# Edge keys kept by feature and turned back, over a longer look-ahead, in a graph attention kernel

## The chip, the cores and the metric

One NeuronCore of a Trainium2 chip runs the whole program. The metric is device time in microseconds (us); less is better. The kernel before took 2671.06 us as the median of three runs (2661.86 to 2672.03).

## The reference, cut to what matters

There are 12500 nodes and 212500 directed edges, sorted by their target node, each with 128 features in float32. Eight heads of 16 features work side by side.

```python
h = jnp.maximum(_layernorm(x, axis=-1), 0.0)
q = (h @ Wq.T + bq).reshape(N, 8, 16)
k = (edge_h @ Wk.T + bk).reshape(-1, 8, 16)          # one k per edge
v = (h @ Wv.T + bv).reshape(N, 8, 16)
qs, qd = q[src], q[dst]
in_m, out_m, diag_m = (jnp.sum(a * b, axis=-1) for a, b in ((qs, k), (qd, k), (qs, qd)))
score = (_segment_softmax(in_m * SCALE, dst, N) + _segment_softmax(out_m * SCALE, dst, N)
         + _segment_softmax(diag_m * SCALE, dst, N)) * distance ** lam
out = segment_sum(score[..., None] * v[dst], dst, N).reshape(N, 128) @ Wo.T + bo
x = x + leaky_relu(out, negative_slope=0.1)
```

## The kernel before, in words

Everything here is in `ordered_path`. A short first stage normalizes the nodes and writes a table of q. Then a loop runs over 415 turns (`for g in range(end)`, L1694), each on 512 edges: 4 edges on each of 128 partitions. Five turns make a step: `s = g % 5`, `t = g // 5`, 83 steps. After the loop a short tail finishes the last nodes. The helper `pin` ties every instruction to the one recorded before it on its engine, so the order of the calls in the program is the order on each engine, and a wait of one instruction holds up all that stand behind it there.

In turn g the work that this change touches is the following.

- `fetch_edges` (L692, queue of SyncE, SP): loads the edge features of one turn, 256 KB, into one of six buffers `ea`, six turns ahead.
- `turn(g + 2)`: TensorE (PE) transposes the four 128x128 blocks of `ea` into PSUM (`eT_ps`, one buffer, L1266); ScalarE (ACT) copies them to `eT` in SBUF (L1268). Features now lie on the partitions.
- `one_hots(g + 3)`: two ACT operations (L703, L704) make the selection matrix `oh` for the targets.
- `project(g + 1)`: four matmuls, each with one block of `eT` as the weights and Wk moving (L1274), and one matmul of three rows that adds bk in bfloat16 parts (L1275), fill `k_ps` (two buffers). Edges lie on the partitions again.
- `spread_q(g + 1)`: four bfloat16 matmuls take the targets' q from a window of the table by `oh` (L1282) into `qd_ps` (two buffers); ACT copies it to `qd` (L1285).
- `logits(g)`: VectorE (DVE) multiplies `qq` by `k_ps` (L1293), `qq` by `qd_ps` (L1294), `qd` by `k_ps` (L1295), and reduces over each head's 16 features (L1296).
- `gather(g + 26)` (L712, GpSimd, called POOL): four indirect DMAs fetch the sources' q into `qq`, 64 KB each. The first of the four waits for the PE instruction noted as `behind[.., 0]`, the last one of `project` a turn earlier; the third waits for `behind[.., 2]`, the last that PE was given in the earlier turn.

Behind these each turn carries a piece of older steps' work, by `s`: transposes of the logits (`turn_head`, `turn_logits`, L1316, L1324), running maxima on DVE (L1356, L1363, L1384) and their transposes (`turn_max`, L1396), exponentials (L1405, L1406, L1424), the selection `sel` (L1438 to L1442), sums per node (`to_rows`, L1452, L1457) and their stores on SP (L1473), and some node work (L1197 to L1241). Below this is called the small work of a turn. `fetch_rows` (L686) loads the window of q; `fetch` (L665, L670) loads 630 KB and 135 KB once a step.

PSUM has eight banks: `eT_ps` 1, `k_ps` 2, `qd_ps` 2 and 3 shared by the small work (`small`).

## Time and profile before

| what | value |
|---|---|
| median of three runs | 2671.06 us |
| profiled execution | 2660.3 us |
| its span, first to last instruction | 2658.5 us |
| mean granted TensorE clock | 0.756 |
| PE busy | 71% of the span |
| weight loads (PEld) busy | 55% |
| DVE busy | 76% |
| ACT busy | 53% |
| POOL busy | 60% |
| mean traffic to and from HBM | 134 GB/s |

A group row of the profile reads: line, engine, operation, what it writes and reads, shape, count; then busy time in us and the mean of one in ns; then how long the engine sat idle just before these instructions, and what ended most of that. PE is the row of matmuls, PEld that of the weight loads that overlap them. The ends of matmuls are modelled and not measured, so their durations overlap. "Remote" as the end of a wait means that the profile names no instruction for it, and "issue" that it shows no wait at all.

### The profile page before, as it was taken

The numbers are of one execution on the slowest core, as the hardware profiler recorded it, in microseconds if no ns is written. First come the engines' busy times: TensorE is split into PE (matmuls) and PEld (weight loads), VectorE is DVE, ScalarE is ACT, GpSimd is POOL, SyncE is SP. The second block draws the span as 40 slices with busy tenths as digits, with TensorE's granted clock in tenths as the row PEclk, the third lists the DMA queues.
The fourth block names the chain that finished last, engine by engine and source line by source line (L and its number), as shares of the span: only waits on it lengthen the run. The fifth ranks groups of instructions, "written<-read, shape, count | busy, mean of one in ns | idle before, by whom it ended". The sixth has DMA issues, their size and how long they took to land.

```text
span 2658.5 us, 37037 instructions
## 1 busy us (share of the span) xinstructions
PE 1895.1 (71%) x10956; PEld 1466.7 (55%) x10956; DVE 2032.3 (76%) x2813; ACT 1406.8 (53%) x2743; POOL 1584.0 (60%) x1680
## 2 busy tenths in 40 slices
PE   4657866677677767777777767767767687777785
PEld 2446655555455555555555556545655565555564
DVE  4648878777777877777778777777877777777995
ACT  3647745554455555554555555545555555554672
POOL 6655666666666666666666666666666666666100
PEclk6777877776777777777777777777777777677886
DMA  7655445445545555455445444554455445454431
GB/s 197 191 163 150 127 133 143 129 135 139 146 131 144 134 147 135 136 141 141 119 130 139 128 129 130 135 137 122 123 140 135 127 127 135 134 131 122 126 88 53
DMA packets 379583, 357.03 MB, mean 134 GB/s; under 512 B 193216, under 2 KB 299371, under 8 KB 379167
## 3 DMA queue, kind: packets, MB, share of 16 engines
q1 hardware_dynamic: 310637, 239.38, 32.5%
q0 software_dynamic: 53152, 108.92, 16.4%
q10 hardware_dynamic: 15584, 6.27, 1.0%
q8 instruction: 90, 1.47, 0.2%
q14 instruction: 120, 0.98, 0.1%
HBM read 322.10 MB, written 32.22 MB: 133 GB/s over the span
## 4 chain that ended last, share of the span: by engine, by line
PE 48%; issue 14%; ACT 14%; DVE 12%; another core or an unknown queue 10%; DMA 1%; DVEq 1%; POOL 0%; SPq 0%; ACTq 0%
PE k_ps L1274 13%; PE eT_ps L1266 8%; PE w_ps L1452 6%; PE qd_ps L1282 4%; PE k_ps L1275 4%; ACT eT L1268 3%; ACT qd L1285 2%; PE m_ps L1396 2%; DVE lT L1296 2%; PE node_ps L1205 2%; ACT relb L703 2%; DVE prod L1294 2%; DVE prod L1293 1%; PE d_ps L1438 1%
## 5 line engine op out<-in xcount | busy, mean ns | idle before, releaser
L712 POOL DMA_INDIRECT qq<-q_table,sources x1564 | 1480.3, 946 | 852.7 <-issue 355.1
L1296 DVE TENSOR_REDUCE lT<-prod 128x96 f32<-128x1536 f32 x415 | 727.5, 1753 | 14.3
L1274 PE MATMUL k_ps<-wk,eT 128*128 128x128 f32 x3320 | 613.6, 343 | 70.5 <-issue 41.0
L1274 PEld LDWEIGHTS k_ps<-wk,eT 128*128 128x128 f32 x3320 | 562.0, 254 | 99.0 <-issue 54.2
L1266 PE MATMUL eT_ps<-ident,ea 128*128 128x128 f32 x1660 | 352.7, 347 | 349.7 <-issue 226.9
L1285 ACT COPY qd<-qd_ps 128x512 f32<-128x512 f32 x415 | 239.4, 577 | 533.7 <-remote 164.3
L1266 PEld LDWEIGHTS eT_ps<-ident,ea 128*128 128x128 f32 x1660 | 243.5, 177 | 441.1 <-issue 269.5
L1293 DVE TENSOR_TENSOR prod<-qq,k_ps 128x512 f32<-128x512 f32 x412 | 280.5, 681 | 186.6 <-remote 55.4
L1268 ACT COPY eT<-eT_ps 128x512 f32<-128x512 f32 x415 | 242.7, 585 | 252.9 <-remote 125.2
L1294 DVE TENSOR_TENSOR prod<-qq,qd_ps 128x512 f32<-128x512 f32 x412 | 281.4, 683 | 100.8 <-ACT qd L1285 55.0
L703 ACT ACTIVATE relb<-relb,before 126x512 bf16<-126x512 bf16 x415 | 302.6, 729 | 0.0
L1295 DVE TENSOR_TENSOR prod<-qd,k_ps 128x512 f32<-128x512 f32 x415 | 282.2, 680 | 0.0
L1452 PE MATMUL w_ps<-back,sel 128*126 128x144 f32 (+1 forms) x1296 | 209.5, 325 | 95.0 <-ACT sel L1442 59.2
L704 ACT ACTIVATE oh<-relb 126x512 bf16<-126x512 bf16 x415 | 261.4, 630 | 13.2
L1452 PEld LDWEIGHTS w_ps<-back,sel 128*126 128x126 f32 (+1 forms) x1296 | 190.7, 218 | 106.0 <-ACT sel L1442 66.2
L1282 PE MATMUL qd_ps<-win,oh 126*128 126x128 bf16 x1660 | 194.8, 248 | 12.6 <-issue 12.4
L1275 PE MATMUL k_ps<-b,ones 3*128 3x512 bf16 x415 | 192.6, 464 | 4.7 <-issue 4.7
L1282 PEld LDWEIGHTS <-oh 126*128 126x128 bf16 x1660 | 109.2, 107 | 141.7 <-issue 141.4
L1405 DVE TENSOR_TENSOR back<-lT,m_ps 128x480 f32<-128x480 f32 x83 | 54.1, 651 | 98.3 <-remote 37.7
L1356 DVE TENSOR_TENSOR_SCAN l_ps<-far,carry,l_ps 120x512 f32<-120x512 bf16 x80 | 102.5, 1282 | 20.1 <-PE h_ps L1324 10.2
L1396 PE MATMUL m_ps<-ident,m 120*128 120x120 f32 x332 | 72.4, 349 | 52.7 <-issue 38.1
L712 POOL DMA_INDIRECT qq<-in_x_dram,sources x84 | 81.7, 973 | 42.8 <-issue 22.2
(237 smaller groups left out, 1811.1 us busy)
## 6 DMA issues: line engine op xcount, KB each, us to landing
ea<-in_edge_attr_dram SPq DMA_DIRECT2D x415, 256.0 KB
relb<-rel_d SPq DMA_DIRECT2D x83, 630.0 KB
qq<-q_table,sources POOLq DMA_INDIRECT x1564
win<-q_table SPq DMA_DIRECT2D x415, 31.5 KB
far<-far_d SPq DMA_DIRECT2D x84, 135.0 KB
q_table<-q SPq DMA_DIRECT2D x24, 384.0 KB
sums<-rows SPq DMA_DIRECT2D x411, 7.9 KB
q_table<-xq SPq DMA_DIRECT2D x24, 256.0 KB
```

Of the source, the lines that this page charges most:

```text
L703: pin(nc.scalar.activation(d, d, AF.Abs, bias=before[:K3]))
L712: rows = pin(nc.gpsimd.indirect_dma_start(out=qq[:, j, :], out_offset=None, in_=x if g < RAW else q_table, in_offset=bass.IndirectOffsetOn ...
L1266: pin(nc.tensor.transpose(eT_ps[:, j, :], eas[g][:, j * F:(j + 1) * F], ident))
L1268: pin(nc.scalar.copy(eT, eT_ps))
L1274: pin(nc.tensor.matmul(k_ps[:, j, :], eTs[g][:, j, :], wk, start=(j == 0), stop=False))
L1275: pin(nc.tensor.matmul(k_ps, ones3, bk3, start=False, stop=True))
L1282: pin(nc.tensor.matmul(qd_ps[:, j, :], ohs[g][:, j * P:(j + 1) * P], d["win"][:, s, :], start=(j == 0), stop=(j == JN - 1)))
L1285: pin(nc.scalar.copy(qds[g], qd_ps))
L1293: pin(nc.vector.tensor_mul(prod[:, :, 0, :], qqs[g], ks[g]))
L1294: pin(nc.vector.tensor_mul(prod[:, :, 1, :], qqs[g], q_ps[g]))
L1296: pin(nc.vector.tensor_reduce(lTs[t][:, :, s, :], prod.rearrange("p j i (h d) -> p j (i h) d", d=DIM), AX.X, ALU.add))
L1452: pin(nc.tensor.matmul(w_ps[:(hi - lo) * W, lo:hi].rearrange("p s c -> p (s c)"), d["sel"][:n, j, lo:hi, :].rearrange("p s w -> p (s w)"), ...
```

## The change

Wk stays in the array as the weights, and the transposed edge features move through it, 512 columns in one matmul. The product is k by feature (`kT_ps`); ACT adds bk as a bias per partition while it copies it to SBUF (`kT`), and PE transposes it back into `k_ps` (`turn_back`). In turn g PE now does `turn_back(g + 1)`, `spread_q(g + 1)`, `project(g + 3)`, `turn(g + 4)` and then the small work. `kT_ps` takes one PSUM bank, and `qd_ps` has one buffer in place of two; the product with `qd_ps` comes first in `logits`. `behind[.., 0]` is now the last instruction of `spread_q`. `eT` has two buffers in place of three. The edge features come in two loads a step, one of three turns (768 KB) and one of two turns (512 KB), with one buffer each, called seven turns ahead, behind `turn(g + 4)`.

```diff
+    bk_col = consts.tile([P, 1], F32, name="bk_col")
+    pin(nc.scalar.dma_start(bk_col, bk[:, None]))
...
+    EA = {0: 3, 3: 2}
...
-    AHEAD, IDX, EDGES = LOOK + FIRST, 8, 6
+    AHEAD, IDX, EDGES = LOOK + FIRST, 8, 7
...
     def fetch_edges(g):
-        if g < end:
-            ea = eas[g] = load.tile([P, JN * F], F32, name="ea", bufs=EDGES)
+        if g < end and g % S in EA:
+            n = EA[g % S]
+            ea = load.tile([P, n, JN * F], F32, name=f"ea_{n}", bufs=1)
+            for i in range(n):
+                eas[g + i] = ea[:, i]
             pin(nc.sync.dma_start(
                 ea, edge_attr[:end * BE, :].rearrange("(s b p j) f -> p s b (j f)", s=S, b=G, p=P)
-                [:, g % S, g // S, :]))
+                [:, g % S:g % S + n, g // S, :]))
...
-            eT = work.tile([P, JN, P], F32, name="eT", bufs=3)
+            eT = work.tile([P, JN, P], F32, name="eT")
...
         def project(g):
+            kT_ps = ps.tile([P, JN, P], F32, name="kT_ps", bufs=1)
+            pin(nc.tensor.matmul(kT_ps.rearrange("f j p -> f (j p)"), wk,
+                                 eTs.pop(g).rearrange("f j p -> f (j p)"), start=True, stop=True))
+            kTs[g] = work.tile([P, JN, P], F32, name="kT", bufs=3)
+            pin(nc.scalar.activation(kTs[g], kT_ps, AF.Identity, bias=bk_col))
+
+        def turn_back(g):
             k_ps = ks[g] = ps.tile([P, JN, F], F32, name="k_ps", bufs=2)
             for j in range(JN):
-                pin(nc.tensor.matmul(k_ps[:, j, :], eTs[g][:, j, :], wk, start=(j == 0), stop=False))
-            pin(nc.tensor.matmul(k_ps, ones3, bk3, start=False, stop=True))
-            del eTs[g]
+                pin(nc.tensor.transpose(k_ps[:, j, :], kTs[g][:, j, :], ident))
+            del kTs[g]
...
-            qd_ps = q_ps[g] = ps.tile([P, JN, F], F32, name="qd_ps", bufs=2)
+            qd_ps = q_ps[g] = ps.tile([P, JN, F], F32, name="qd_ps", bufs=1)
...
+            pin(nc.vector.tensor_mul(prod[:, :, 1, :], qqs[g], q_ps[g]))
             pin(nc.vector.tensor_mul(prod[:, :, 0, :], qqs[g], ks[g]))
-            pin(nc.vector.tensor_mul(prod[:, :, 1, :], qqs[g], q_ps[g]))
...
         for g in range(end):
...
-            fetch_edges(g + EDGES)
             if s == 1:
                 load_sources(t + IDX)
-            if g + 2 < end:
-                turn(g + 2)
-            one_hots(g + 3)
             if g + 1 < end:
-                project(g + 1)
+                turn_back(g + 1)
+                one_hots(g + 3)
+                spread_q(g + 1)
                 behind[g + 1, 0] = pinned[products]
-                spread_q(g + 1)
+            if g + 3 < end:
+                project(g + 3)
+            if g + 4 < end:
+                turn(g + 4)
+            fetch_edges(g + EDGES)
             logits(g)
```

What it does to the order on the engines is shown at three places; line numbers in rows of the changed kernel are its own. On PE before, from the last part of one `spread_q` through the next turn's transposes of `ea` and its `project` into the next `spread_q`:

```order
L1282 LDWEIGHTS oh_12237
L1282 MATMUL qd_ps_12355<-win_11957,oh_12237 128x128
L1266 MATMUL eT_ps_12378<-ident_75,ea_12166 128x128 x4
L1274 MATMUL k_ps_12388<-wk_94,eT_12344 128x128 x4
L1275 LDWEIGHTS ones3_90
L1275 MATMUL k_ps_12388<-b3_96,ones3_90 128x512
L1282 LDWEIGHTS oh_12291
L1282 MATMUL qd_ps_12394<-win_11957,oh_12291 128x128
```

The `eT` that `project` reads was transposed one turn earlier, and the transposes into the one `eT_ps` stand ahead of it. On PE now, at a like place in a turn whose small work is `show_ends` (L1450):

```order
L1294 LDWEIGHTS oh_12460
L1294 MATMUL qd_ps_12551<-win_12054,oh_12460 128x128
L1279 MATMUL kT_ps_12558<-eT_12521,wk_96 128x512
L1272 MATMUL eT_ps_12562<-ident_75,ea_3_12297 128x128 x4
L1450 LDWEIGHTS ends_t1_113
L1450 MATMUL d_ps_12577<-shows_111,ends_t1_113 128x420
L1287 MATMUL k_ps_12608<-ident_75,kT_12514 128x128 x4
L1294 LDWEIGHTS oh_12502
L1294 MATMUL qd_ps_12616<-win_12328,oh_12502 128x128
```

`spread_q` (L1294) moved ahead of the transposes of `ea` (L1272), and what DVE needs of k (L1287) is read from a `kT` that was projected two turns earlier. On ACT before, from one copy of `qd` to the next, in a turn with the exponential (L1406) and node work (L1186) in it:

```order
L1285 COPY qd_9714<-qd_ps_9709 128x512
L1406 ACTIVATE back_9726<-back_9726 128x20x24
L1186 ACTIVATE h_9731<-x_in_9640,shift_98,inv_97 128x128 x2
L1268 COPY eT_9746<-eT_ps_9741 128x512
L703 ACTIVATE relb_9516<-relb_9516,before_88 126x512
L704 ACTIVATE oh_9748<-relb_9516 126x512
L1285 COPY qd_9762<-qd_ps_9757 128x512
```

And on ACT now, through one turn:

```order
L709 ACTIVATE relb_8415<-relb_8415,before_90 126x512
L710 ACTIVATE oh_8656<-relb_8415 126x512
L1297 COPY qd_8664<-qd_ps_8659 128x512
L1282 ACTIVATE kT_8668<-kT_ps_8666,bk_col_78 128x512
L1274 COPY eT_8675<-eT_ps_8670 128x512
L1453 ACTIVATE sel_8684<-d_ps_8685 128x420
```

Three copies out of PSUM now follow each other, and the small work stands behind the copy of `eT` in place of ahead of it. On the queue of SP now, in a turn with s = 3, where the load of three turns stands (before, a load of one turn stood in every turn, ahead of the window `win` and the stores of `sums`):

```order
L689 DMA win_10662<-q3_table_62 126x128
L1485 ISA
L1485 DMA sums3_68<-rows_10713 42x48
L698 DMA ea_3_10928<-in_edge_attr_128_dram 128x3x512
L668 DMA relb_10944<-rel_d_63 126x5x512
L673 DMA far_10946<-far_d_64 120x1x576
L675 TENSOR_LOAD places_120
```

The load of `ea_3` waits for the transposes of the same turn, and the once-a-step loads of `fetch` queue behind it.

More of the change, by code (lines that the diff above doesn't have):

```diff
@@ L1690, in ordered_path @@
         project(0)
+        turn(1)
+        turn_back(0)
         spread_q(0)
-        turn(1)
+        project(1)
+        turn(2)
+        project(2)
+        turn(3)
+        fetch_edges(S)
         raw_rectify(SOON)
@@ L1810, in ordered_path @@
             halves_of(ab, engine)
[L1811 to L1813 removed]
+        places_o = [ps.tile([P, JN, F], F32, name=name, bufs=n) for name, n in
+                    (("eT_ps", 1), ("kT_ps", 1), ("k_ps", 2), ("k_ps", 2), ("qd_ps", 1))]
         for r in range(len(rest) + 2):
```

9 lines of the change are left out of this document (3 added, 6 removed).

## The prediction, made before the changed kernel was timed

> **What bounds the kernel now.** I read the busy rows of the page first, then the same by stretches, with and without the gathers of POOL.
>
> ```profile
> PE 1895.1 (71%) x10956; PEld 1466.7 (55%) x10956; DVE 2032.3 (76%) x2813; ACT 1406.8 (53%) x2743; POOL 1584.0 (60%) x1680
> ```
>
> No engine is full over the span. The stretches say more. The first view counts the reduces of `logits` (L1296), one for each turn; the second shows what all engines do in the same stretches.
>
> ```profile
> 300.00:1350.00 1050.00, 312.04 (x178) 0.75 0.52 137
> ...
> 2480.00:2590.00 110.00, 42.07 (x24) 0.86 0.36 101
> ```
>
> ```profile
> 300.00:1350.00 1050.00, 756.79 (x4325) 578.79 (x4323) 817.44 (x1018) 545.11 (x1037) 671.63 (x710) 0.75 0.52 137
> ...
> 2480.00:2590.00 110.00, 92.84 (x627) 73.52 (x627) 107.69 (x136) 80.55 (x163) 1.67 (x4) 0.86 0.36 101
> ```
>
> A turn takes 1050/178 = 5.90 us while POOL gathers and 110/24 = 4.58 us once the gathers are over. In the later stretch DVE is busy for 107.69 of 110 us: there DVE is the bound. In the earlier one DVE is busy for 817.44/178 = 4.59 us of 5.90 and PE for 4.25 us: some 1.3 us a turn are waits, over about 390 turns 510 us. Who waits is in the rows of the page's costliest groups and, for POOL, in the first of them.
>
> ```profile
> L712 POOL DMA_INDIRECT qq<-q_table,sources x1564 | 1480.3, 946 | 852.7 <-issue 355.1
> ...
> L1274 PE MATMUL k_ps<-wk,eT 128*128 128x128 f32 x3320 | 613.6, 343 | 70.5 <-issue 41.0
> L1274 PEld LDWEIGHTS k_ps<-wk,eT 128*128 128x128 f32 x3320 | 562.0, 254 | 99.0 <-issue 54.2
> L1266 PE MATMUL eT_ps<-ident,ea 128*128 128x128 f32 x1660 | 352.7, 347 | 349.7 <-issue 226.9
> L1285 ACT COPY qd<-qd_ps 128x512 f32<-128x512 f32 x415 | 239.4, 577 | 533.7 <-remote 164.3
> L1266 PEld LDWEIGHTS eT_ps<-ident,ea 128*128 128x128 f32 x1660 | 243.5, 177 | 441.1 <-issue 269.5
> L1293 DVE TENSOR_TENSOR prod<-qq,k_ps 128x512 f32<-128x512 f32 x412 | 280.5, 681 | 186.6 <-remote 55.4
> L1268 ACT COPY eT<-eT_ps 128x512 f32<-128x512 f32 x415 | 242.7, 585 | 252.9 <-remote 125.2
> L1294 DVE TENSOR_TENSOR prod<-qq,qd_ps 128x512 f32<-128x512 f32 x412 | 281.4, 683 | 100.8 <-ACT qd L1285 55.0
> ...
> L1282 PE MATMUL qd_ps<-win,oh 126*128 126x128 bf16 x1660 | 194.8, 248 | 12.6 <-issue 12.4
> L1275 PE MATMUL k_ps<-b,ones 3*128 3x512 bf16 x415 | 192.6, 464 | 4.7 <-issue 4.7
> ```
>
> PE's one large wait stands ahead of the transposes into `eT_ps`: 349.7 us. ACT waits 533.7 us ahead of the copy of `qd` and 252.9 us ahead of the copy of `eT`, and DVE 186.6 + 100.8 = 287.4 us ahead of its first two products. The timeline of one turn shows how they hang together.
>
> ```profile
> 1517.82 0.60 PE L1282 MATMUL qd_ps<-win,oh 126*128 126x128 bf16 x4
> ...
> 1518.21 1.06 PE L1266 MATMUL eT_ps<-ident,ea 128*128 128x128 f32 x4
> ...
> 1518.84 0.94 POOL L712 DMA_INDIRECT qq<-q_table,sources  x1 [0.30 <-issue]
> ...
> 1521.05 0.69 PE L1396 MATMUL m_ps<-ident,m 120*128 120x120 f32 x4
> ...
> 1522.42 0.69 DVE L1293 TENSOR_TENSOR prod<-qq,k_ps 128x512 f32<-128x512 f32 x1 [1.92 <-PE m_ps L1396]
> 1522.48 0.59 ACT L1285 COPY qd<-qd_ps 128x512 f32<-128x512 f32 x1 [4.44 <-PE m_ps L1396]
> 1522.66 0.94 POOL L712 DMA_INDIRECT qq<-q_table,sources  x1 [1.63 <-PE m_ps L1396]
> ...
> 1522.96 0.59 ACT L1268 COPY eT<-eT_ps 128x512 f32<-128x512 f32 x1
> ...
> 1523.61 1.12 PE L1266 MATMUL eT_ps<-ident,ea 128*128 128x128 f32 x4 [1.86 <-ACT eT L1268]
> ```
>
> By the records `spread_q` ends at 1518.42, but its copy starts at 1522.48, with ACT idle for 4.44 us: what PE has done reaches DVE, ACT and POOL some 4 us late, and to all three at once. Then ACT copies `eT`, and only then can PE transpose again. This lateness goes with the gathers. The copy of `qd` by stretches, first the one with gathers, then the one without:
>
> ```profile
> L1285 ACT COPY qd<-qd_ps 128x512 f32<-128x512 f32 x355 | 205.1, 578 | 493.9 <-remote 138.8 <-PE qd_ps L1282 78.3 <-PE m_ps L1396 76.0
> ...
> L1285 ACT COPY qd<-qd_ps 128x512 f32<-128x512 f32 x24 | 13.7, 570 | 1.6 <-PE qd_ps L1282 1.5
> ```
>
> 493.9/355 = 1.39 us of idle a turn against 1.6/24 = 0.07 us. The trace doesn't say why PE's releases come late while gathers run; I take it as given. The loop is then a round of late releases, PE to ACT to PE, and looser couplings should shorten it.
>
> **The change part by part.** Times are those of the profiled execution, 2660.3 us with a span of 2658.5.
>
> *PE's work.* It loses the rows of L1274 and L1275, 613.6 + 192.6 = 806.2 us. It gains 415 x 4 transposes, by the row of L1266 352.7 us, and 415 matmuls of 512 columns, in two records each. The nearest row is a float32 matmul of that shape:
>
> ```profile
> L1572 PE MATMUL rest_ps<-q_in,ident 128*128 128x512 f32 (+1 forms) x34 | 21.2, 712 | 2.9 <-issue 2.5 <-ACT hT L1200 0.4
> ```
>
> 21.2/34 = 0.62 us a record gives 830 x 0.62 = 515 us. Net: 515 + 353 - 806 = +62 us. If a record takes its whole 0.712 us it is +138, if the bias matmul's overlap was worth nothing it is about 0. Weight loads fall by 562.0 us and gain 243.5 and some 160, but they overlap and are no term. PE's share of the chain that ended last is this:
>
> ```profile
> PE 48%; issue 14%; ACT 14%; DVE 12%; another core or an unknown queue 10%; DMA 1%; DVEq 1%; POOL 0%; SPq 0%; ACTq 0%
> ```
>
> At 48% the +62 cost 30 us; bounds 0 and 138.
>
> *ACT's work.* 415 more copies at 0.585 us (L1268): +243 us, 53% to 62% of the span. They lie beside other work except where PE or DVE wait for ACT; at ACT's 14% of the chain that is +34 us, bounds 0 and 243.
>
> *The wait ahead of the transposes.* The wait rows of PE have it in two parts.
>
> ```profile
> PE eT_ps L1266 <- issue: 226.9, 132, 7.4
> ...
> PE eT_ps L1266 <- ACT eT L1268: 110.3, 65, 6.3
> ```
>
> 197 waits hold nearly all of 349.7 us: 1.77 us each. Nothing of the next turn may pass them now. After the change PE meets `turn_back` first, whose `kT` was made two turns earlier: 352.7/415 = 0.85 us of work that needs nothing fresh. Then `spread_q` (194.8/415 = 0.47 us), which needs the product and the copy that free the one `qd_ps`, and those come as late as the copy of `eT` did. So I count 0.85 of each 1.77 us as covered and the rest as still there, now ahead of `spread_q`, `project` or `turn`: 197 x 0.85 = -167 us. Bounds: none of it, or both pieces, 197 x 1.32 = -260. What is late next is `qd_ps`.
>
> *Edits at nothing.* The new order of the three products costs nothing, as all three are done before the reduce; it frees `qd_ps` one product earlier. A load fewer in three of five turns on SP's queue saves nothing (SPq is 0% of the chain). The load of three turns waits on SP for the transposes of its own turn, with `relb`, `far`, the window and the stores behind it; the transposes that need it stand three turns later, 3 x 5.90 = 17.7 us, which hide it. If that cover goes, PE waits for the load (a rival below). `eT` with two buffers: its reader is one turn behind, so 0. POOL's first gate moves from behind `project` to behind `spread_q`, one piece earlier in PE's turn: taken as 0, at best a part of POOL's wait. `bk_col` is one small load at the start: 0.
>
> Sum: -167 + 30 + 34 = -103, so 2557 for the profiled execution. The median of the runs lies 10.8 us above that execution: **2568 us**. About 0.5% (13 us) is what a measurement of this kernel can tell from no change.
>
> **A rule that speaks against it.** Rows first: the clock was 0.75 in the stretch where PE was busy for 72% and 0.86 where it was for 84%. The Trainium skill ("TensorE: Matmul & The Clock Gate", Part 4: PE-mode transpose) holds that work in transpose mode does not count as activity for the gate, so that the full clock is not granted for it. By that rule this change, which swaps matmuls for transposes, would lower the clock; the trace shows the clock rising with PE's busy share, but no stretch with transposes alone.
>
> **The rivals.**
>
> *The gain is larger.* `turn_back` and `spread_q` both run ahead of the late releases, PE is never the one waited for, and DVE's waits shrink too: -260 + 30 + 34 = -196, so 2475. For it: DVE has 4.59 us of work in 5.90, and POOL's own pace, 946 ns (L712) and 0.30 us between two gathers (the timeline's row of 1518.84), is 4 x 1.25 = 5.0 us a turn. Against it: the single `qd_ps`. Chance 0.15.
>
> *The clock falls.* The clock goes down to half in stretches of some us:
>
> ```profile
> 1513.20:1519.90 6.70, 6.14 (x30) 5.19 (x30) 5.75 (x9) 4.42 (x10) 4.72 (x5) 0.50 0.54 158
> ```
>
> Suppose that L1266's 353 us of transposes count for nothing, and that the clock goes linearly from 0.5 at no counted work to its 0.756 now. Counted work falls from 1895 - 353 = 1542 us to 1957 - 706 = 1251, the clock to 0.708, and PE's 1957 us grow by 7%, 134 us, of which 48% is 64 us: 2632. For it: the rule above. Against: the rows above, where a busier PE got more clock. Chance 0.05.
>
> *The gathers set the pace.* POOL runs until PE's late release stops it, and the lateness ends when it stops; then the order on PE matters little and a turn stays at 5.90 us: 2671, within 0.5%. For it: the two rows of `qd` by stretch. Chance 0.12.
>
> *Slower: the single `qd_ps`.* Now `spread_q(g + 1)` waits for the first product of turn g and the copy of `qd`, and the first product of turn g + 1 waits for it: product 0.68 us, `spread_q` 0.47, 0.1 to hand over (the copy of `eT` ends at 1523.55, PE starts at 1523.61), and the lateness, which two buffers used to hide for a turn. With the 4.06 us of the timeline (1518.42 to 1522.48) the round is 5.3 us and hidden; but single waits for `qd` were longer.
>
> ```profile
> ACT qd L1285 <- remote: 164.3, 55, 8.3
> ...
> ACT qd L1285 <- PE qd_ps L1282: 89.7, 32, 5.0
> ACT qd L1285 <- PE m_ps L1396: 76.0, 18, 4.8
> ACT qd L1285 <- PE eT_ps L1266: 65.0, 40, 4.6
> ...
> ACT qd L1285 <- PE k_ps L1275: 29.7, 12, 4.9
> ```
>
> In these 157 turns ACT stood waiting for `spread_q`. If each now pays the serial 0.68 + 0.47 + 0.1 = 1.25 us, that is +196 us: 2568 + 196 = 2764. It decides from 103 us of new wait, 0.25 us a turn. Chance 0.26.
>
> *Slower: the features come late.* One buffer for three turns: its load starts only when PE's late release reaches SP, and SP may be held by a store of sums.
>
> ```profile
> SPq L1473 <- ACT rows L1457: 443.8, 70, 18.5
> ```
>
> The longest such wait, 18.5 us, is above the 17.7 us of cover. If each of the 83 loads makes PE wait 2 us more, that is +166: 2734. Chance 0.06.
>
> **How the numbers follow.** The forecast keeps 0.36. Faster by over 0.5%: 0.36 + 0.15 + 0.05 = 0.56; within 0.5%: 0.12; slower: 0.26 + 0.06 = 0.32. The likeliest case's own range goes from 2504 (both costs hidden, -167) to 2651 (the cover half as good, -84 + 64 = -20). For 8 in 10 the range must hold most of both slower cases and most of the larger gain: 2440 to 2780.
>
> **What would show it.** Right: the idle time ahead of the transposes of `ea` falls from 349.7 to under 200 us, the new `kT` and `k_ps` groups have 515 and 353 us, a turn with gathers takes about 5.65 us, DVE's waits ahead of its products fall below 287 us. Wrong: the idle time ahead of `spread_q`, 12.6 us now, rises above 300 us with the first product as what ended it (the single buffer); or PE waits for the load of `ea_3` every fifth turn; or the clock goes to 0.71; or the stretch without gathers leaves 4.58 us a turn.

## The result, and the profile after

The change made the kernel a little slower: 2682.51 us as the median of 13 runs (2673.19 to 2690.04), beside 2667.64 us for the kernel before (13 runs, 2660.04 to 2672.75). The ratio is 1.0057, 95% interval 1.0045 to 1.0068: 15 us, or 0.57%, just past the 0.5% that I had set as the bound. The profiled execution took 2676.7 us with a span of 2674.9 us.

The experiments ran in groups, each with the kernel before on the same chip, and in some groups the kernel before took 2665 to 2668 us as here (the *high level*), in others 2186 to 2189 us (the *low level*), with all runs of a group alike; so every kernel is compared only with the kernel before of its own group.

The busy row of the page after, and the two stretches of the prediction by engine:

```profile
PE 1797.9 (67%) x9711; PEld 1250.9 (47%) x9711; DVE 2020.4 (76%) x2813; ACT 1658.0 (62%) x3158; POOL 1583.8 (59%) x1680
```

```profile
300.00:1350.00 1050.00, 714.94 (x3797) 487.64 (x3798) 807.92 (x1015) 653.08 (x1220) 668.54 (x706) 0.81 0.50 136
...
2480.00:2590.00 110.00, 83.17 (x531) 59.92 (x530) 103.93 (x131) 88.93 (x170) 7.68 (x11) 0.93 0.39 111
```

PE is 97 us less busy over the span and ACT 251 us more, and the granted clock rose from 0.75 to 0.81. POOL does the same work at the same pace. The costliest groups show where the waits went:

```profile
L718 POOL DMA_INDIRECT qq<-q_table,sources x1564 | 1481.6, 947 | 863.0 <-issue 373.5
...
L1279 PE MATMUL kT_ps<-eT,wk 128*128 128x512 f32 x830 | 601.2, 814 | 138.7 <-ACT eT L1274 77.6
L1294 PE MATMUL qd_ps<-win,oh 126*128 126x128 bf16 x1660 | 187.8, 242 | 580.0 <-DVE prod L1305 297.0
L1297 ACT COPY qd<-qd_ps 128x512 f32<-128x512 f32 x415 | 238.4, 574 | 353.7 <-remote 188.4
...
L1305 DVE TENSOR_TENSOR prod<-qq,qd_ps 128x512 f32<-128x512 f32 x412 | 280.4, 681 | 180.6 <-issue 81.8
...
L1282 ACT ACTIVATE kT<-kT_ps,bk_col 128x512 f32<-128x512 f32 x415 | 286.7, 691 | 116.8 <-remote 35.5
...
L1272 PE MATMUL eT_ps<-ident,ea 128*128 128x128 f32 x1660 | 325.0, 331 | 3.8 <-DVE att_t L874 2.8
...
L1287 PE MATMUL k_ps<-ident,kT 128*128 128x128 f32 x1660 | 294.5, 306 | 1.8 <-issue 1.8
...
L1417 DVE TENSOR_TENSOR back<-lT,m_ps 128x480 f32<-128x480 f32 x83 | 54.2, 653 | 207.6 <-remote 86.1
```

The wait ahead of the transposes of `ea` is gone: 349.7 us before, 3.8 us now. It stands ahead of `spread_q` instead, 580.0 us where there were 12.6. ACT waits less (353.7 us ahead of the copy of `qd`, 533.7 before), DVE waits less ahead of its products (180.6 us, 287.4 before) and as much more ahead of `back`, its subtraction of the running maxima (207.6, 98.3 before). POOL waits 863.0 us, 852.7 before.

The most telling view is the count of reduces (L1296 before, L1308 after), one a turn, in three stages: up to the 51st, the next 330, and the rest. First before, then after.

```profile
0.00:475.30 475.30, 89.40 (x51) 0.76 0.57 156
475.30:2429.80 1954.50, 578.48 (x330) 0.75 0.50 133
2429.80:2658.50 228.70, 59.60 (x34) 0.80 0.34 96
```

```profile
0.00:485.80 485.80, 89.39 (x51) 0.83 0.56 154
485.80:2440.50 1954.70, 578.45 (x330) 0.81 0.49 133
2440.50:2674.90 234.40, 59.60 (x34) 0.81 0.32 91
```

In the middle stage 330 turns take 1954.5 us before and 1954.7 us after, 5.923 us each: the order of the work on PE changed and in this pair of profiles the pace did not move by 0.1%. Of the 16.4 us of span nearly all are lost at the two ends, 10.5 us in the first stage and 5.7 in the last. (A second pair of profiles, from `e6_before_same` and `e5_after_same` below, has 477.0, 1957.9 and 231.2 us before, and 484.2, 1962.8 and 232.6 after. There the middle stage is 4.9 us longer, 0.25%. One execution differs from the next by some us in each stage, so the split of the 15 us over the stages is rough; the first stage is longer after in both pairs.)

### The profile page after: what moved, and what is told of

Its sections match the earlier page's. It is cut to its first block, busy times and chain, and to the rows that moved or that the text cites. A ratio compares the mean times of both kernels' runs of the same rounds, so it can differ in the third digit from the quotient of the medians.

```text
span 2674.9 us, 34598 instructions
## 1 busy us (share of the span) xinstructions
PE 1797.9 (67%) x9711; PEld 1250.9 (47%) x9711; DVE 2020.4 (76%) x2813; ACT 1658.0 (62%) x3158; POOL 1583.8 (59%) x1680
## 4 chain that ended last, share of the span: by engine, by line
PE 27%; DVE 27%; issue 14%; ACT 12%; another core or an unknown queue 9%; POOL 3%; DVEq 3%; DMA 3%; SPq 1%; ACTq 0%; POOLq 0%
PE kT_ps L1279 9%; DVE lT L1308 6%; DVE prod L1305 5%; PE eT_ps L1272 4%; DVE prod L1307 3%; DVE prod L1306 3%; POOL qq L718 3%; PE qd_ps L1294 3%; DVEq L1305 3%; PE w_ps L1464 2%; DVE m L1396 2%; DVE l_ps L1368 2%; PE k_ps L1287 2%; ACT relb L709 2%
## 5 line engine op out<-in xcount | busy, mean ns | idle before, releaser
L718 POOL DMA_INDIRECT qq<-q_table,sources x1564 | 1481.6, 947 | 863.0 <-issue 373.5
L1308 DVE TENSOR_REDUCE lT<-prod 128x96 f32<-128x1536 f32 x415 | 727.4, 1753 | 14.3
L1279 PE MATMUL kT_ps<-eT,wk 128*128 128x512 f32 x830 | 601.2, 814 | 138.7 <-ACT eT L1274 77.6
L1294 PE MATMUL qd_ps<-win,oh 126*128 126x128 bf16 x1660 | 187.8, 242 | 580.0 <-DVE prod L1305 297.0
L1297 ACT COPY qd<-qd_ps 128x512 f32<-128x512 f32 x415 | 238.4, 574 | 353.7 <-remote 188.4
L1294 PEld LDWEIGHTS <-oh 126*128 126x128 bf16 x1660 | 132.1, 108 | 646.5 <-issue 339.4
L1272 PEld LDWEIGHTS eT_ps<-ident,ea 128*128 128x128 f32 x1660 | 271.1, 176 | 318.1 <-issue 305.7
L1305 DVE TENSOR_TENSOR prod<-qq,qd_ps 128x512 f32<-128x512 f32 x412 | 280.4, 681 | 180.6 <-issue 81.8
L1282 ACT ACTIVATE kT<-kT_ps,bk_col 128x512 f32<-128x512 f32 x415 | 286.7, 691 | 116.8 <-remote 35.5
L1272 PE MATMUL eT_ps<-ident,ea 128*128 128x128 f32 x1660 | 325.0, 331 | 3.8 <-DVE att_t L874 2.8
L1287 PE MATMUL k_ps<-ident,kT 128*128 128x128 f32 x1660 | 294.5, 306 | 1.8 <-issue 1.8
L1287 PEld LDWEIGHTS k_ps<-ident,kT 128*128 128x128 f32 x1660 | 223.8, 160 | 32.7 <-issue 22.5
L1279 PEld LDWEIGHTS kT_ps<-eT,wk 128*128 128x128 f32 x830 | 158.0, 237 | 166.2 <-ACT eT L1274 88.6
L1417 DVE TENSOR_TENSOR back<-lT,m_ps 128x480 f32<-128x480 f32 x83 | 54.2, 653 | 207.6 <-remote 86.1
L1464 PE MATMUL w_ps<-back,sel 128*126 128x144 f32 (+1 forms) x1296 | 166.0, 284 | 15.9 <-ACT sel L1453 6.0
L1464 PEld LDWEIGHTS w_ps<-back,sel 128*126 128x126 f32 (+1 forms) x1296 | 159.7, 188 | 21.4 <-ACT sel L1454 7.4
```

The costliest lines, as they stand in the source:

```text
L718: rows = pin(nc.gpsimd.indirect_dma_start(out=qq[:, j, :], out_offset=None, in_=x if g < RAW else q_table, in_offset=bass.IndirectOffsetOn ...
L1272: pin(nc.tensor.transpose(eT_ps[:, j, :], eas[g][:, j * F:(j + 1) * F], ident))
L1279: pin(nc.tensor.matmul(kT_ps.rearrange("f j p -> f (j p)"), wk, eTs.pop(g).rearrange("f j p -> f (j p)"), start=True, stop=True))
L1282: pin(nc.scalar.activation(kTs[g], kT_ps, AF.Identity, bias=bk_col))
L1287: pin(nc.tensor.transpose(k_ps[:, j, :], kTs[g][:, j, :], ident))
L1294: pin(nc.tensor.matmul(qd_ps[:, j, :], ohs[g][:, j * P:(j + 1) * P], d["win"][:, s, :], start=(j == 0), stop=(j == JN - 1)))
```

## The experiments

Two theories stood at the start. **G**: while POOL gathers, PE's releases are seen late, and this sets 5.92 us a turn whatever the order on PE. **Q**: the new order did win time, and the single `qd_ps` took it back.

### The gathers taken away

The edit, in both kernels; the rows then come in order and not by `src`, so the output is not the reference's:

```python
 if g >= AHEAD:                       # from turn 29 on
     lo = (g % 24) * JN * P
     pin(nc.sync.dma_start(qq, q_table[lo:lo + JN * P, :].rearrange("(p j) f -> p j f", j=JN)))
     return
```

First at the low level, where it could show little:

> The kernel before, but the features of q of turn 29 and on are not gathered by src: each turn loads 512 rows of the table that stand in order, in one load on SP's queue, so POOL has no gathers in the loop (the output is not the reference's; bytes and all other work are the same). Theory G (the gathers set the pace: while they run, what PE has done is seen late, and a turn takes 5.92 us whatever the order on PE): the lateness goes, the idle time ahead of the copy of qd falls from 1.39 us a turn to under 0.15, a turn takes about 4.6 us as at the end of the loop, and the kernel takes about 2670 - 386 x 1.3 = 2170 us. Rival W (the waits are in the round of PE, ACT and DVE itself, with the gathers beside it): a turn stays above 5.5 us, over 2500 us.

> The changed kernel with the same edit: rows in order instead of gathers from turn 29 on (output not the reference's). Theory G: a turn takes about 4.6 us here too, within 2% of the kernel before with the same edit (2150 to 2200 us). Theory Q (the new order did win time, and the single qd_ps, which now waits for DVE's first product, takes it back): the wait of PE ahead of spread_q stays near 1.4 us a turn without gathers, the turn stays above 5.3 us and the time 5% or more above the kernel before with this edit.

Measured: 2127.98 us for the kernel before with the edit (called e1 below), 0.9727 of the kernel before (0.9709 to 0.9746), and 2173.06 us for the changed one (e2), 0.9943 (0.9927 to 0.9960). The kernel before with its gathers took 2186.42 us there, so that group had little to lose and could not decide between G and Q. It did show that without gathers the changed kernel is the slower one, by 45 us. Then at the high level:

> The kernel before with rows in order instead of gathers from turn 29 on (output not the reference's), for a chip on which the kernel before takes about 2667 us. Theory G (while POOL gathers, what PE has done is seen late): without gathers the turn goes from 5.92 to about 4.6 us and the time to 2130 to 2200 us, as on the chip where the kernel before took 2186. Rival C (that chip's PE releases are late by themselves, gathers or not): a turn stays above 5.5 us, over 2500 us. Where the kernel before is near 2186 us, 2128 again.

> The changed kernel with rows in order (output not the reference's). Theory G with theory D (without lateness DVE is the bound, and the single qd_ps makes it wait a little): 2150 to 2200 us on either chip, 1.5 to 2.5% above the kernel before with the same edit. Rival C: over 2500 us on a chip where the kernel before takes about 2667.

Measured: 2153.36 us for the kernel before with the edit (e9), 0.8083 (0.8069 to 0.8096), and 2200.80 us for the changed one (e10), 0.8260 (0.8246 to 0.8273). The middle stage of the two, 330 turns each:

```profile
429.50:1930.90 1501.40, 578.41 (x330) 0.84 0.59 173
```

```profile
446.40:1976.10 1529.70, 578.42 (x330) 0.90 0.59 170
```

A turn takes 1501.4/330 = 4.550 us before and 1529.7/330 = 4.635 us after. ACT's wait ahead of the copy of `qd`, 533.7 us with gathers, shrinks in the kernel before:

```profile
L1289 ACT COPY qd<-qd_ps 128x512 f32<-128x512 f32 x415 | 236.6, 570 | 78.4 <-PE qd_ps L1286 63.6
```

So at the high level the gathers cost 1.37 us a turn, and with them goes the lateness: G's numbers came as expected (2200.80 us lies 0.8 above its range), rival C fell. And without gathers the change costs 47 us. PE still waits 462.3 us ahead of `spread_q` there, 1.11 us a turn, not far from what theory Q had expected, but the turn is 4.635 us and not above 5.3: that wait costs little. In the kernel before DVE hardly waits for anyone; in the changed one DVE itself waits, as its wait rows between 450 and 1900 us show, first the kernel before (L1297 is the product with `k_ps`, L1298 the one with `qd_ps`), then the changed one (L1309 is the product with `qd_ps`, L1421 `back`; the inserted lines move the numbers by four):

```profile
DVE prod L1297 <- PE k_ps L1279: 1.3, 2, 0.7
DVE prod L1298 <- ACT qd L1289: 0.9, 2, 0.5
```

```profile
DVE back L1421 <- PE m_ps L1412: 14.8, 21, 1.0
DVE prod L1309 <- ACT qd L1301: 9.8, 12, 0.8
```

The transposes of `m` stand behind `spread_q` on PE, which waits for DVE's first product, so `back` gets its `m_ps` late; and the first product waits for ACT's copy of `qd`.

The traces also show the lateness itself, over many turns. Take the copies of `qd` after 500 us (to 2400 us, or to 1900 in the shorter runs) ahead of which ACT stood idle for over 0.2 us. They start 4.72 us behind the recorded end of their own `spread_q` in the median before the change and 3.60 us after it, but 0.04 us in e9, and 0.04 us in each single one. Of the semaphore updates that are recorded for PE, 36% before and 35% after come within 0.1 us of the update before, none in e9; and 56% and 58% fall into POOL's pauses of over 0.4 us, which make up 19% of the time. So while POOL gathers at this level, PE's updates are seen late, and many come in bursts, the larger part of them in POOL's pauses.

### The single qd_ps

Two kernels free `spread_q` from DVE in two ways. In the first, DVE's first product reads ACT's copy:

```diff
-            pin(nc.vector.tensor_mul(prod[:, :, 1, :], qqs[g], q_ps[g]))
+            pin(nc.vector.tensor_mul(prod[:, :, 1, :], qqs[g], qds[g]))
```

> The changed kernel, but DVE's first product reads qd from ACT's copy in SBUF and no longer from qd_ps; so spread_q(g + 1) has to wait for ACT's copy of qd alone, which is done before the first product starts. Theory Q: the idle time of PE ahead of spread_q falls from 580 to under 200 us, and 100 us or more come back: 2560 to 2600 us. Theory G: the turn keeps its 5.92 us, the wait moves to another place, and the time stays within 0.5% of 2682 us.

> The changed kernel with DVE's first product reading qd from ACT's copy, so that spread_q no longer waits for DVE. Where the kernel before takes about 2667 us: theory G, a turn stays at 5.9 us and the time within 0.5% of 2682, PE's wait moving from spread_q to turn_back (behind DVE's third product) or project; theory Q, 2560 to 2620 us. Where it takes about 2186: 2230 again, 2.5% above the kernel before with gates, because DVE's first product then stands behind ACT's copy.

Measured at the low level (e3) 2230.12 us, 1.0200 (1.0183 to 1.0217); at the high level (e11) 2674.49 us, 1.0039 (1.0025 to 1.0054). PE's wait ahead of `spread_q` did fall, to 238.0 us at the high level, and part of it went to the next matmul:

```profile
L1279 PE MATMUL kT_ps<-eT,wk 128*128 128x512 f32 x830 | 597.8, 809 | 376.6 <-ACT eT L1274 179.4
...
L1294 PE MATMUL qd_ps<-win,oh 126*128 126x128 bf16 x1660 | 186.4, 241 | 238.0 <-issue 156.6
```

```profile
482.90:2437.90 1955.00, 578.43 (x330) 0.81 0.48 133
```

The turn stayed at 1955.0/330 = 5.924 us. Theory Q's 2560 to 2620 us was far off; of the 8 us below the changed kernel nothing is certain, as the intervals of the two ratios overlap. At the low level this kernel is 2% slower than the kernel before (the changed kernel itself was not run there). PE waits for DVE's third product ahead of `turn_back`,

```profile
PE k_ps L1287 <- DVE prod L1307: 285.7, 187, 5.9
```

and the trace names what DVE lacks: it waits 41.8 us for gathered rows (13.8 us in e4, below). In e3 a gather takes 977 ns, in e4 949; 1564 gathers of 28 ns more are 44 us, an estimate of the size of the loss. POOL makes no pause of over 0.4 us there between 500 and 2100 us, and the turn grows from 4.6 us (500/108) between 500 and 1000 us to 5.2 us (500/96) between 1500 and 2000: the loop has used up its look-ahead and follows POOL.

In the second, `eT_ps` and `kT_ps` share a bank, `qd_ps` has two, and `project` stands ahead of `spread_q` (the calls of a turn are put in one line here, and the tail's list of the same tiles is left out):

```diff
-eT_ps = ps.tile([P, JN, P], F32, name="eT_ps", bufs=1)
-kT_ps = ps.tile([P, JN, P], F32, name="kT_ps", bufs=1)
-qd_ps = ps.tile([P, JN, F], F32, name="qd_ps", bufs=1)
+eT_ps = ps.tile([P, JN, P], F32, name="eT_ps", tag="T_ps", bufs=1)
+kT_ps = ps.tile([P, JN, P], F32, name="kT_ps", tag="T_ps", bufs=1)
+qd_ps = ps.tile([P, JN, F], F32, name="qd_ps", bufs=2)
...
-turn_back(g + 1); one_hots(g + 3); spread_q(g + 1); project(g + 3); turn(g + 4)
+turn_back(g + 1); one_hots(g + 3); project(g + 3); spread_q(g + 1); turn(g + 4)
```

> The changed kernel with the banks dealt otherwise: eT_ps and kT_ps share one, qd_ps has two as before the change, and PE's order in a turn is turn_back, project, spread_q, turn. Theory Q (the single qd_ps costs time): PE's idle time ahead of spread_q falls from 580 us (or 492, where a turn is 4.6 us) to under 100 us, and the time falls below the changed kernel's by 1 to 3%. Theory G: under 0.5% apart where a turn is 5.92 us. Rival S (the shared bank puts ACT's copy of kT between two pieces of PE's turn): PE waits 0.3 us or more a turn ahead of the transposes of ea, and the time is not below the changed kernel's.

Measured at the high level (e7): 2831.32 us, 1.0626 (1.0607 to 1.0645).

```profile
L1272 PE MATMUL eT_ps<-ident,ea 128*128 128x128 f32 x1660 | 337.3, 337 | 695.9 <-ACT kT L1282 517.7
...
L1294 PE MATMUL qd_ps<-win,oh 126*128 126x128 bf16 x1660 | 185.5, 241 | 0.0
```

```profile
520.00:2571.10 2051.10, 578.52 (x330) 0.80 0.46 127
```

The wait ahead of `spread_q` went to nothing and the kernel got slower: now PE needs ACT's answer within one turn (`kT_ps` out, `kT` copied, bank free), 517.7 us of waits, and a turn is 2051.1/330 = 6.215 us. Rival S held. The order and the banks on PE are thus not without effect: a tighter round lengthens the turn. But neither of the two looser orders that ran at this level, the change and e11, shortened it below 5.92 us.

### The gates

In either kernel, gathers from turn 29 on no longer wait for PE:

```diff
-                held = behind.get((g - LOOK, j), held)
+                held = held if g < AHEAD else None
```

> The changed kernel without the two gates a turn that hold POOL's gathers behind PE (they carry no data; the buffers of qq still hold a gather back until the products that read its place are done). Theory G, as far as it goes: POOL runs on without its pauses until the buffers stop it, PE's work is seen later than now, and the time is above 2682 us, 2700 to 2900. Rival P (POOL's pauses, about 0.93 us a turn at the gates, are what the turn is made of: 4 gathers of 1.25 us and the pause): without gates the turn goes towards 5.0 to 5.3 us, 2320 to 2450 us.

> The changed kernel without the gates, for a chip on which the kernel before takes 2667 us and without its gates 2904. Theory R (the looser order does make the loop less sensitive to late releases; with gates that is hidden, because POOL's pace is tied to PE's): it loses less than the kernel before does, 2680 to 2800 us. Theory N (the order does not matter for late releases either way): about 2904 + 15, 2880 to 2940 us. Where the kernel before takes 2186: 2187 again.

> The kernel before without the two gates a turn that hold POOL behind PE. Rival P (the gates' pauses make the turn): 1.5% or more faster than the kernel before; where the kernel before is near 2668 us, 10% or more. Theory D (DVE is the bound where a turn is 4.6 us): within 1% there. Theory G, where the kernel before is near 2668 us: PE's work is seen later still, and it is slower.

Both runs of the changed kernel, e4 and e15, fell on the low level, for which e4's expectation gave no figure and e15's said 2187 again: 2186.83 us, 1.0005 (0.9995 to 1.0014), and 2191.55 us, 1.0009 (0.9995 to 1.0023). The kernel before, e8, ran at the high level: 2903.90 us, 1.0897 (1.0873 to 1.0920), with

```profile
L712 POOL DMA_INDIRECT qq<-q_table,sources x1564 | 1490.4, 953 | 1076.0 <-DVE prod L1294 523.8
...
L1285 ACT COPY qd<-qd_ps 128x512 f32<-128x512 f32 x415 | 239.3, 577 | 672.6 <-remote 456.6
```

Rival P fell: POOL without its gates waits longer, 1076.0 us, now 523.8 of them for the products that free its buffers, and ACT's wait for `qd` rises from 533.7 to 672.6 us. Between 500 and 2400 us POOL now does 8.9 gathers from one pause of over 0.4 us to the next, where it did 6.1, a pause is 3.6 us long in place of 1.7, and 65% of PE's updates come in these pauses. Whether the looser order would lose less without gates stayed open, as e15 was not at the high level.

Four gates a turn, one for each gather, were to make POOL's runs of gathers shorter:

```diff
                 turn_back(g + 1)
+                behind[g + 1, 0] = pinned[products]
                 one_hots(g + 3)
                 spread_q(g + 1)
-                behind[g + 1, 0] = pinned[products]
+                behind[g + 1, 1] = pinned[products]
...
+            behind[g + 1, 2] = pinned[products]
...
-            behind[g + 1, 2] = pinned[products]
+            behind[g + 1, 3] = pinned[products]
```

> The changed kernel with four gates a turn in place of two: each of the four gathers waits for another point of PE's turn (behind turn_back, behind spread_q, behind turn, and at the turn's end), so that POOL gathers one at a time, not four to eight in a row. Theory G, in this form: PE's work is seen when POOL pauses; shorter runs of gathers make the lateness shorter, and where the kernel before takes about 2667 us this takes 2400 to 2600. Rival P2 (each gate costs a pause of its own, 0.5 to 0.9 us): two gates more make the turn 1 to 1.8 us longer, over 3000 us. Where the kernel before takes about 2186 us: within 1% of the changed kernel.

Measured at the high level (e12): 2683.50 us, 1.0066 (1.0050 to 1.0083), the changed kernel's own time.

```profile
486.80:2449.40 1962.60, 578.41 (x330) 0.81 0.48 133
```

1962.6/330 = 5.947 us a turn. Both expectations missed. The edit hardly made the runs shorter, 5.2 gathers from pause to pause where the changed kernel has 5.9, so short runs were not tested. The median lateness of the copies of `qd`, counted as above, is 2.91 us here, 3.60 in the changed kernel and 5.18 in e11, and the turn is 5.92 to 5.95 us in all three: the pace does not follow the lateness of this one release.

### Half the gathers, and the same kernels again

Half the gathers: two rows of four by index, the other two in order (output not the reference's).

> The changed kernel with two gathers a turn instead of four from turn 29 on; the other two rows of each partition come in order by a load on SP's queue (output not the reference's). Theory G as a sum (a turn is the gathers' own time, 1.25 us each, and POOL's pause of about 0.93 us, unless DVE's 4.64 us are longer): 2 x 1.25 + 0.93 is below 4.64, so 2200 to 2260 us. Rival L (a release is late by a fixed time whenever gathers run at all): a turn stays above 5.3 us, over 2450 us. Where the kernel before takes 2186: about 2175.

This too fell on the low level, 2176.51 us, 0.9949 (0.9932 to 0.9965), and could not decide there. Whether fewer gathers make the lateness shorter is open.

> The changed kernel as it is, on the chip of this call. The first four runs stood beside a kernel before of 2186 us, not 2668: on that chip PE's work is seen at once although POOL gathers, and a turn is 4.6 us. If that holds again, theory D (DVE is the bound there, and the single qd_ps costs what it makes DVE wait, as in the two kernels with rows in order, 2173 against 2128 us) expects 2185 to 2235 us against 2186, 0 to 2% slower. Where the kernel before is near 2668 us again, theory G (the late releases set a pace of 5.92 us whatever PE's order) expects 2682, 0.3 to 0.8% slower. Rival: on a chip without the lateness the looser order on PE shows its gain, over 1% faster.

> The kernel before as it is, for its profile on the chip of this call. Where its time is near 2186 us, theory G (lateness of what PE has done) expects the idle time ahead of the copy of qd to have gone from 533.7 to under 100 us, POOL's idle time from 853 to under 520 us, and DVE busy for over 90%; where it is near 2668 us, the rows as they were. Rival (a slower engine or a slower memory on one of the chips): the mean time of one gather, product or reduce differs between the chips by 5% or more, and the waits keep their place.

At the high level the changed kernel took 2682.05 us, 1.0063 (1.0048 to 1.0079), and the kernel before 2667.90 us in a single run, with the rows as they were (538.5 us of idle time ahead of the copy of `qd`): the result stands.

### Where the 15 us are lost

Without gathers the changed kernel is slower. First the order on PE, in the changed kernel (the calls of a turn in one line):

```diff
-turn_back(g + 1); one_hots(g + 3); spread_q(g + 1); project(g + 3); turn(g + 4)
+turn_back(g + 1); one_hots(g + 3); project(g + 3); turn(g + 4); spread_q(g + 1)
```

> The changed kernel with PE's order in a turn changed from turn_back, spread_q, project, turn to turn_back, project, turn, spread_q. The wait for DVE's first product then stands behind project and turn, not ahead of them. Theory G with H (the 15 us are lost only where the gathers do not set the pace, in the first 50 turns and the last 25, by the single qd_ps that holds up the rest of PE's turn): a turn in between stays 5.92 us, and 5 to 15 us come back: 2667 to 2677 where the kernel before takes 2667. Rival A (the added work of ACT, 243 us, and of PE costs the 15 us): within 3 us of the changed kernel, 2679 to 2685.

> The same order with rows in order instead of gathers from turn 29 on (output not the reference's). Theory H: DVE's waits ahead of back and of its first product go, a turn falls from 4.635 to about 4.56 us, and the time from 2201 to 2155 to 2175 us (on a chip where the kernel before takes 2186: from 2173 to 2130 to 2145). Rival A: within 10 us of 2201 (2173).

Both fell on the low level: 2195.33 us (e13), 1.0030 (1.0020 to 1.0041), and 2184.45 us (e14), 0.9984 (0.9974 to 0.9993). The changed kernel itself was not run there, so e13 has nothing beside it but the kernel before. e14 stands beside e2, 0.9943: it is slower by 0.4%, not faster. DVE's waits between 450 and 1900 us, first of e2, then of e14:

```profile
DVE back L1421 <- PE m_ps L1412: 15.8, 21, 1.2
DVE prod L1309 <- ACT qd L1301: 9.7, 12, 0.8
```

```profile
DVE prod L1309 <- ACT qd L1301: 38.0, 38, 2.7
```

The wait ahead of `back` went as theory H said, but the one ahead of the first product grew by more. H fell as I had put it, and pointed at that product. In all 415 turns of the traces of before, after, e1, e2 and e14, the product with `qd_ps` starts only when ACT's copy of the same `qd_ps` has ended, 0.03 us later at the earliest. Before, the product with `k_ps` stood ahead and covered at least part of this. So the new order of the products alone, on the kernel before:

```diff
-            pin(nc.vector.tensor_mul(prod[:, :, 0, :], qqs[g], ks[g]))
             pin(nc.vector.tensor_mul(prod[:, :, 1, :], qqs[g], q_ps[g]))
+            pin(nc.vector.tensor_mul(prod[:, :, 0, :], qqs[g], ks[g]))
```

and the two loads of edge features alone (`EA`, `ea_3` and `ea_2` as in the change, fetched five turns ahead behind `turn(g + 2)`):

> The kernel before with the new order of the products alone: DVE multiplies with qd_ps first, with k_ps second. Theory H2 (the product with qd_ps starts only when ACT's copy of qd has ended; standing first, it has no product ahead of it that covers this wait): where the gathers do not set the pace DVE waits 0.05 to 0.2 us a turn more, 4 to 12 us in all where the kernel before takes 2667, 10 to 40 us where it takes 2187. Rival K (the order of the products is free, as the prediction had it, and the cost is that of the single qd_ps and of the added work): within 3 us of the kernel before.

> The kernel before with edge features in two loads for five turns (three turns, two turns, one buffer each), at the look-ahead of before. Theory F (the features come late): the first load of a step can start only when the third turn's transposes are seen done, and PE waits ahead of the transposes in every fifth turn; 8 us or more slower. Rival K: the load is hidden, as the prediction had it; within 3 us of the kernel before on either chip, with SP's waits for the puts of sums gone from the top.

Measured at the high level: 2674.69 us for the order of the products (e17), 1.0037 (1.0023 to 1.0051), and 2666.49 us for the two loads (e18), 1.0010 (1.0000 to 1.0019). The page of e17 has, where before had 186.6 and 100.8 us ahead of the two products,

```profile
L1293 DVE TENSOR_TENSOR prod<-qq,qd_ps 128x512 f32<-128x512 f32 x412 | 280.8, 681 | 326.8 <-ACT qd L1285 238.9
...
L1294 DVE TENSOR_TENSOR prod<-qq,k_ps 128x512 f32<-128x512 f32 x412 | 279.8, 679 | 0.0
```

and its stages are

```profile
0.00:484.10 484.10, 89.40 (x51) 0.81 0.57 154
484.10:2436.60 1952.50, 578.46 (x330) 0.73 0.50 133
2436.60:2669.50 232.90, 59.60 (x34) 0.77 0.33 94
```

The order of the products alone costs the kernel before 0.37%, about 10 us. Against the first profile of before it costs them where the change does: 8.8 us in the first stage (10.5 for the whole change), none in the middle, 4.2 in the last (5.7); against the second profile, `e6_before_same`, it is 7.1, none and 1.7. H2 held, rival K fell for the products. For the two loads K's time held, but not its sign: SP's waits for the stores of `sums` stayed on top, 514.9 us where there were 443.8. The 5 us that are left of 15 are within what the intervals allow; whether they are the single `qd_ps` or the added work was not settled.

No version that computes the reference's output beat the kernel before at the high level.

## Why the prediction was wrong, point by point

**The step that failed** is the one on the wait ahead of the transposes: "So I count 0.85 of each 1.77 us as covered", -167 us. That wait did go, and by more than I had counted, 345.9 us; but it was not what the turn was waiting for. PE's wait moved whole to `spread_q`, and 330 turns took 1954.7 us for 1954.5: the term was worth nothing, not -167. I took the lateness of PE's releases as given and treated the turn as a round PE to ACT to PE that a looser order shortens. The runs showed a pace that holds under six arrangements (before, after, e11, e12, e17, e18: 5.917 to 5.947 us), and that goes with the gathers (4.550 and 4.635 us without). How the late releases and POOL's gates add up to just 5.92 us was not shown: four gathers of 0.95 us and the 0.30 us behind each are 5.0 us, and POOL's longer pauses are the rest. The row to have believed was the one I used for the rival: 493.9 us of idle time in 355 turns with gathers against 1.6 in 24 without.

How the lateness looks after the change, in the timeline of the same place as in the prediction:

```profile
1518.28 0.94 POOL L718 DMA_INDIRECT qq<-q_table,sources  x1 [0.30 <-issue]
...
1518.34 0.39 PE L1294 MATMUL qd_ps<-win,oh 126*128 126x128 bf16 x4
...
1520.88 0.94 POOL L718 DMA_INDIRECT qq<-q_table,sources  x1 [1.66 <-PE eT_ps L1272]
...
1522.33 0.57 ACT L1297 COPY qd<-qd_ps 128x512 f32<-128x512 f32 x1
1522.79 0.69 ACT L1282 ACTIVATE kT<-kT_ps,bk_col 128x512 f32<-128x512 f32 x1
...
1523.67 0.38 PE L1294 MATMUL qd_ps<-win,oh 126*128 126x128 bf16 x4 [1.08 <-issue]
```

By the records `spread_q` ends at 1518.73, its copy starts at 1522.33: 3.60 us. For the first half of that ACT stands idle, until a burst of PE's updates from 1520.53 on; for the second it does node work and the two operations of `one_hots`, which stand ahead of the copy. POOL pauses once, 1.66 us, as before the change, and the next `spread_q` starts 5.33 us after the last. The Trainium skill ("Perfetto Trace Analysis", Summary: the profiler window per engine type) says that the time until a semaphore update is seen lies outside the window that the profile shows for TensorE, and that the end shown is an estimate; it gives no duration. The trace agrees that the recorded end alone does not tell when a consumer may start: it was 0.04 us later in e9 and 3.60 us in the median here. No run here showed what delays the update.

**PE's work**, +62 us: as a sum of rows it was right to a few tenths (601.2 + 325.0 + 294.5 = 1220.7 us for 613.6 + 192.6 + 352.7 = 1158.9), but only because two errors cancelled: the wide matmuls took 601 us, not 515, and the transposes 619.5, not 705. Its lower bound, "about 0", follows from no row. PE's busy time as a whole fell by 97 us all the same, as rows that the change does not touch got shorter, with the granted clock up from 0.756 to 0.813 (L1452, now L1464: 209.5 to 166.0 us); how much of that is the clock's was not worked out. Nor does Wk stay loaded over the turns: its loads are 830, two a turn, 158.0 us on PEld. The price of 30 us was wrong: in the middle stage of the first pair of profiles the work cost nothing. **ACT's work**, +243 us: it grew by 251 us; its price of 34 us was wrong in the same way.

**Edits at nothing**: right for the loads (e18). Wrong for the products: "costs nothing, as all three are done before the reduce" forgot that the one put first waits for ACT's copy. In the kernel before that alone is 10 us (e17); if it is the same in the changed kernel, it is 10 of the 15 us.

**The rivals.** That the gathers set the pace, chance 0.12, is the one that the runs bear out: the turn kept its length, and the gathers' going shortened it. Its 2671 us are 0.4% below what was measured, the products' order and what is left being on top. The single `qd_ps`, 0.26, put the wait in the right place and with the right ender (580.0 us, 297.0 by the first product) and gave it a price, 196 us, that it does not have, for e11 takes the wait for DVE away and the turn stays. The features did not come late: PE waits 3.8 us ahead of the transposes. The clock did not fall; it went from 0.756 to 0.813 although the transposes' rows grew from 352.7 to 619.5 us. The Trainium skill's rule that PE-mode transposes do not count for the clock gate ("TensorE: Matmul & The Clock Gate", Part 4) is not borne out by this trace, which has, though, no stretch of transposes alone.

**What I had named as signs** did not separate right from wrong. Two signs of being wrong came: the wait ahead of `spread_q` above 300 us with the first product as its end, and the stretch without gathers leaving 4.58 us a turn (its 110 us hold 40.52 us of reduces after, 42.07 before: 4.76 us a turn). But so did two signs of being right: the wait ahead of the transposes fell under 200 us, and DVE's waits ahead of its products under 287. Waits that move say little; the length of a turn with gathers, 5.92 us and not 5.65, was the sign that decided.

## What to carry to other kernels

A wait that is long on one engine is not yet a cost: before pricing it, compare a stage with and without the suspected pacemaker, here turns with and without gathers, and ask whether the turn would end sooner if that wait were gone. If waits on every engine vanish together in the stage without it, expect a new order on one engine to move the wait and not the end, as it did here. And of several operations that a later one needs, the one to stand first is the one whose inputs are ready first, even when all must be done.

## What the runs showed of the hardware

- The same program has two levels: the kernel before took 2186 to 2189 us in some groups of runs and 2665 to 2668 in others, and the chip recorded as number 5 gave both. A gather takes 945 to 953 ns in both (e3 and e11 apart). Without gathers the two levels nearly meet: a turn of the kernel before is 1503.1/330 = 4.555 us at the low one (e1) and 4.550 at the high one (e9). At the low level, with gates and gathers (e13), POOL's waits are mostly the 0.30 us between gathers and ACT hardly waits:

```profile
L718 POOL DMA_INDIRECT qq<-q_table,sources x1564 | 1485.7, 950 | 509.3 <-issue 319.6
...
L1297 ACT COPY qd<-qd_ps 128x512 f32<-128x512 f32 x415 | 246.9, 595 | 40.6 <-PE qd_ps L1294 35.7
```

 The copies of `qd` for which ACT stood idle start 0.04 us behind the recorded end of `spread_q` there. So PE's releases are late while POOL gathers at the high level, and prompt at the low one. What makes the difference was not found.
- At the low level POOL's own pace, 0.95 us and 0.30 us for each of four gathers, 5.0 us a turn, is longer than DVE's 4.6 us. The loop can be faster than POOL only as long as its look-ahead of 26 turns lasts: in e13, 330 turns take 1550.9 us, 4.70 us each, and the last gather starts at 2121.0 of 2195.5 us.
- With the first product reading both its operands from SBUF (e3, e11), a gather took 977 and 970 ns in the mean instead of 949 (e4) and 947 (after). Why was not tested.
